# Reordering the start of a two-layer graph attention kernel: weight copies, bias sums and row terms

## The chip, the cores and the metric

The kernel runs on one core of a Trainium2 chip. A core has five engines with instruction streams of their own: TensorE (PE in the profile, its weight loads PEld), VectorE (DVE), ScalarE (ACT), GpSimd (POOL) and SyncE (SP), which here only issues transfers. The metric is device time in microseconds, the median of the runs. An engine runs its instructions in the order in which the built program holds them; that order is made by a scheduler from the order of the source, the tiles' dependencies and the number of buffers, so moving a line in the source can move others too.

## The reference, cut to what matters

Two layers over N = 4096 nodes of width 512. Layer 0 is attention within graphs of 128 nodes, with the dense matrix `adj` added to the scores. Layer 1 is graph attention with 8 heads over the nonzero entries of `adj`.

```python
h = jnp.maximum(_layernorm(x), 0.0)
query = h @ Wq.T + bq;  key = h @ Wk.T + bk;  value = h @ Wv.T + bv
a = jnp.where(mask, query @ key.T * scale, 0.0)
scores = (a + adj + adj) * jnp.where(mask, 1.0, -1000000.0)
x = x + (softmax(scores) * mask) @ value
h = jnp.maximum(_layernorm(x), 0.0)
mx = jnp.einsum('nf,hfd->hnd', h, W)          # layer 1: logits s_i + t_j,
# ... softmax over adj > 0, weighted sum of mx, added to x
```

The kernel folds query and key: `query @ key.T` equals `h M h.T` plus a term for each row and one for each column, with M = Wq.T Wk and with the sums `u` (of Wq and bk), `c` (of Wk and bq) and `z` (of bq and bk). Only M, c, u and z are used afterwards.

## The kernel before

The parts that the change and the prediction touch, with cuts marked. First the folding of the weights:

```python
def fold(sb, tmp, work, ps_t, ps_p):
    wkT_sb = load_weight(tmp, wkT, "wkT_sb", KC, tag="lo")     # four pieces each
    wqT_sb = load_weight(tmp, wqT, "wqT_sb", KC, tag="lo")
    for n, wT in enumerate((wkT_sb, wqT_sb)):
        w = tmp.tile([P, KC, D], F32, name=f"w{n}", tag="lo")
        for k in range(KC):
            pt = ps_t.tile([P, KC, P], F32, name="pt")          # 3 buffers
            for m in range(KC):
                nc.tensor.transpose(pt[:, m, :], wT[:, k, ts(m, P)], ident)   # L174
            dst = w[:, :, ts(k, P)]
            if k % 2: nc.vector.tensor_copy(dst, pt)            # L177
            else:     nc.scalar.copy(dst, pt)                   # L179
    # ...
    for m in range(KC):                                         # M, L190 and L193
        pp = ps_p.tile([P, D], F32, name="pp")                  # 4 buffers
        for k in range(KC):
            nc.tensor.matmul(pp, wq[:, k, ts(m, P)], wk[:, k, :], ...)
        nc.scalar.mul(m_sb[:, m, :], pp, SCALE)
    for n, b in enumerate((bk_sb, bq_sb)):                      # bias rows, L198 and L203
        # pp[:, ts(k, P)] = b[:, k] spread over all partitions, by four products
        row = work.tile([P, D], F32, name=f"b_row{n}", tag="hn")
        nc.scalar.copy(row, pp)
    for dst, wT, row in ((u_col, wqT_sb, rows[0]), (c_sb, wkT_sb, rows[1])):
        for k in range(KC):                                     # bias sums, L208
            nc.vector.scalar_tensor_tensor(wb, wT[:, k, :], SCALE, row, ..., accum_out=dst[:, k:k+1])
    # zp; then u_col spread to u_sb (L218, L222), zp to z_sb (L224, L225)
```

Then the attention loop. It works on groups of two 128-row tiles; `adj` comes in 64 tiles of 128 x 2048 through seven buffers, and each is read by VectorE (a byte mask, L136, stored for layer 1) and by ScalarE (an exponential with a sum, `junk`, L441):

```python
def normed(g):                                  # x -> hT, and the row terms r
    for t in range(G):
        hn = sb.tile([P, D], F32, name="hn")    # 2 buffers; b_row uses the same ones
        norm(xg[g][:, t, :], hn)                # L114, L116, L118, L120, L121
        relu_T(ps_t, hn, hT[:, :, ts(t, P)])    # 4 transposes L127, ScalarE L128
        hu = sb.tile([P, D], BF16, name="hu", bufs=1)
        nc.vector.scalar_tensor_tensor(hu, hn, 0.0, u_sb, ALU.max, ALU.mult,
                                       accum_out=r[:, t : t + 1])      # L394
    nc.gpsimd.tensor_scalar(r, r, z_sb, None, ALU.add)
# before the loop: load_pair(0), wv, bv, adj 0 to 3, load_pair(1), adj 4 to 6;
# normed(0), values(hT, t) L418, read (L136, L441) of group 0, queries(hT) L406, normed(1)
for g in range(NG):
    load_pair(g + 2)                            # x, 3 buffers
    s = scores(g, hT, gT, r, *look)             # L464, exp of s on ScalarE L471
    ngT = queries(nhT)                          # L406
    sT = turned(s)                              # L483, copy to sT on ScalarE L485
    for t in range(G):
        look_on(t)                              # adj of group g + 1
        attend(sT, vs[t], g, t)                 # L491, x1 stored
        nvs.append(values(nhT, t))              # L418
    nhT, nr = normed(g + 2)
# (the last group differs: it prepares layer 1's first rows instead)
```

A stage that prepares layer 1's rows (`project1`, L244) follows, and then 32 aggregations (L284), which take most of the time.

Of the kernel before, what the change touches and what calls it, by code (L numbers as in the profile page):

```python
# [9 lines left out]
F32 = mybir.dt.float32  # L10
# [10 lines left out]
P = 128  # L21
N = 4096
D = 512
NT = N // P
KC = D // P
# [16 lines left out]
SCALE = float(D) ** -0.5  # L42
# [9 lines left out]
def kernel(  # L52
# [22 lines left out]
    nc = tc.nc  # L75
# [11 lines left out]
    ident = const.tile([P, P], F32, name="ident")  # L87
    make_identity(nc, ident)
    one = const.tile([P, 1], F32, name="one")
# [3 lines left out]
    bq_sb = const.tile([P, KC], F32, name="bq_sb")  # L93
    nc.scalar.dma_start(bq_sb, bq)
    bk_sb = const.tile([P, KC], F32, name="bk_sb")
# [15 lines left out]
    def norm(src, hn):  # L111

        stats = small.tile([P, 6], F32, name="stats")
        nc.vector.bn_stats(stats, src)  # L114
        mv = small.tile([P, 2], F32, name="mv")
        nc.vector.bn_aggr(mv, stats)  # L116
        ve = small.tile([P, 1], F32, name="ve")
        nc.gpsimd.tensor_scalar(ve, mv[:, 1:2], EPS, None, ALU.add)  # L118
        rstd = small.tile([P, 1], F32, name="rstd")
        nc.gpsimd.tensor_tensor(rstd, ve, neghalf, ALU.pow)  # L120
        nc.vector.tensor_scalar(hn, src, mv[:, 0:1], rstd, ALU.subtract, ALU.mult)  # L121

    def relu_T(ps_pool, hn, dst):

        pt = ps_pool.tile([P, KC, P], F32, name="pt")
        for k in range(KC):
            nc.tensor.transpose(pt[:, k, :], hn[:, ts(k, P)], ident)  # L127
        nc.scalar.activation(dst, pt, AF.Relu)  # L128
# [11 lines left out]
    def load_weight(pool, src, name, pieces=1, **kw):  # L140
        t = pool.tile([P, KC, D], F32, name=name, **kw)
        n = KC // pieces
        for k in range(0, KC, n):
            nc.sync.dma_start(
                t[:, k : k + n], src[k * P : (k + n) * P].rearrange("(k p) m -> p k m", p=P)
            )
        return t
# [15 lines left out]
    def fold(sb, tmp, work, ps_t, ps_p):  # L163


        wkT_sb = load_weight(tmp, wkT, "wkT_sb", KC, tag="lo")
        wqT_sb = load_weight(tmp, wqT, "wqT_sb", KC, tag="lo")
        nat = []
        for n, wT in enumerate((wkT_sb, wqT_sb)):
            w = tmp.tile([P, KC, D], F32, name=f"w{n}", tag="lo")  # L170
            for k in range(KC):
                pt = ps_t.tile([P, KC, P], F32, name="pt")
                for m in range(KC):
                    nc.tensor.transpose(pt[:, m, :], wT[:, k, ts(m, P)], ident)  # L174
                dst = w[:, :, ts(k, P)]
                if k % 2:
                    nc.vector.tensor_copy(dst, pt)  # L177
                else:
                    nc.scalar.copy(dst, pt)  # L179
            nat.append(w)  # L180
        wk, wq = nat
        m_sb = sb.tile([P, KC, D], F32, name="m_sb")
        c_sb = sb.tile([P, KC], F32, name="c_sb")
        u_col = sb.tile([P, KC], F32, name="u_col")
        u_sb = sb.tile([P, D], F32, name="u_sb")
        z_sb = sb.tile([P, 1], F32, name="z_sb")
        for m in range(KC):
            pp = ps_p.tile([P, D], F32, name="pp")
            for k in range(KC):
                nc.tensor.matmul(  # L190
                    pp, wq[:, k, ts(m, P)], wk[:, k, :], start=(k == 0), stop=(k == KC - 1)
                )
            nc.scalar.mul(m_sb[:, m, :], pp, SCALE)  # L193
        rows = []
        for n, b in enumerate((bk_sb, bq_sb)):
            pp = ps_p.tile([P, D], F32, name="pp")
            for k in range(KC):
                nc.tensor.matmul(  # L198
                    pp[:, ts(k, P)], b[:, k : k + 1].to_broadcast([P, P]), ident,
                    start=True, stop=True,  # L200
                )
            row = work.tile([P, D], F32, name=f"b_row{n}", tag="hn")
            nc.scalar.copy(row, pp)  # L203
            rows.append(row)
        for dst, wT, row in ((u_col, wqT_sb, rows[0]), (c_sb, wkT_sb, rows[1])):
            for k in range(KC):
                wb = work.tile([P, D], BF16, name="wb", tag="hu", bufs=1)
                nc.vector.scalar_tensor_tensor(  # L208
                    wb, wT[:, k, :], SCALE, row, ALU.mult, ALU.mult, accum_out=dst[:, k : k + 1]
                )  # L210
        zk = sb.tile([P, KC], F32, name="zk")
        zp = sb.tile([P, 1], F32, name="zp")
        nc.vector.scalar_tensor_tensor(
            zk, bq_sb, SCALE, bk_sb, ALU.mult, ALU.mult, accum_out=zp
        )
        pp = ps_p.tile([P, D], F32, name="pp")
        for k in range(KC):
            nc.tensor.matmul(  # L218
                pp[:, ts(k, P)], u_col[:, k : k + 1].to_broadcast([P, P]), ident,
                start=True, stop=True,  # L220
            )
        nc.scalar.copy(u_sb, pp)  # L222
        pp = ps_p.tile([P, D], F32, name="pp")
        nc.tensor.matmul(pp[:, :1], zp.to_broadcast([P, P]), one, start=True, stop=True)  # L224
        nc.scalar.copy(z_sb, pp[:, :1])  # L225
        return m_sb, c_sb, u_sb, z_sb

    def split(e, dst):
# [5 lines left out]
    def load_row(pool, i):  # L234
        row = pool.tile([P, D], F32, name="row1")
        nc.sync.dma_start(row, x1_d[ds(i, 1)].rearrange("o p d -> (o p) d"))
        return row
# [104 lines left out]
    with ExitStack() as straight:  # L342
# [4 lines left out]
        with ExitStack() as prep:  # L347
            ps_t = prep.enter_context(tc.tile_pool(name="ps_t0", bufs=3, space=PSUM))
            ps_p = prep.enter_context(tc.tile_pool(name="ps_p0", bufs=4, space=PSUM))
# [28 lines left out]
            with (  # L378
# [5 lines left out]
                def normed(g):  # L384


                    hT = sb.tile([P, KC, G * P], F32, name="hT")
                    r = sb.tile([P, G], F32, name="r", bufs=3)
                    for t in range(G):
                        hn = sb.tile([P, D], F32, name="hn")  # L390
                        norm(xg[g][:, t, :], hn)
                        relu_T(ps_t, hn, hT[:, :, ts(t, P)])
                        hu = sb.tile([P, D], BF16, name="hu", bufs=1)
                        nc.vector.scalar_tensor_tensor(  # L394
                            hu, hn, 0.0, u_sb, ALU.max, ALU.mult, accum_out=r[:, t : t + 1]
                        )
                    nc.gpsimd.tensor_scalar(r, r, z_sb, None, ALU.add)
                    return hT, r
# [105 lines left out]
                NG = NT // G  # L504
                xg, aa = {}, {}
                m_sb, c_sb, u_sb, z_sb = fold(wp, lo, sb, ps_t, ps_p)
                load_pair(0)
                wv = load_weight(wp, wvT, "wv")
# [4 lines left out]
                for k in range(4, AB):  # L513
                    aa[k] = load_adj(ap, k)
                hT, r = normed(0)
                vs = [values(hT, t) for t in range(G)]
                look = seen()
                for t in range(G):
                    look[2].append(read(t, look[0][:, t, :], look[1][t]))
                gT = queries(hT)  # L520
                nhT, nr = normed(1)
                ahead = []
                for g in range(NG):
# [34 lines left out]
                    if g + 2 < NG:  # L558
                        nhT, nr = normed(g + 2)
# [5 lines left out]
            n = len(ahead)  # L565
# [22 lines left out]
        for i in range(NT):  # L588
            row = sb3.tile([P, D], F32, name="row3", bufs=1)
# [29 lines left out]
    with tc.tile_pool(name="ps_ok", bufs=1, space=PSUM) as ps:  # L619
        all_held = small.tile([P, 1], F32, name="all_held")  # L620
        nc.vector.tensor_reduce(all_held, held, AX.X, ALU.min)
        pt = ps.tile([P, P], F32, name="pt_ok")
# [7 lines left out]
    with tc.If(bad > 0):  # L630
# [5 lines left out]
        with (  # L636
# [27 lines left out]
            wq = load_weight(wp, wqT, "wq")  # L664
            wk = load_weight(wp, wkT, "wk")
            wv = load_weight(wp, wvT, "wv")
            with tc.For_i(0, NT, 1) as i:
                row = sb.tile([P, D], F32, name="row")
# [4 lines left out]
                for dst_d, w, b in ((qT_d, wq, bq_sb), (kT_d, wk, bk_sb)):  # L673
                    dst = sb.tile([P, KC, P], F32, name="qk")
                    for m in range(KC):
                        pp = ps_p.tile([P, D], F32, name="pp")
                        for k in range(KC):
                            nc.tensor.matmul(
                                pp[:, :P], w[:, k, ts(m, P)], hT[:, k, :],
                                start=(k == 0), stop=(k == KC - 1),  # L680
# [8 lines left out]
                pp = ps_p.tile([P, D], F32, name="pp")  # L689
# [8 lines left out]
        with (  # L698
# [10 lines left out]
            with tc.For_i(0, NT, 1) as i:  # L709
# [8 lines left out]
                for c in range(N // CW):  # L718
# [12 lines left out]
                    f = sb.tile([P, CW], F32, name="f")  # L731
# [9 lines left out]
                for c in range(N // CW):  # L741
                    v = sb.tile([P, CW // P, D], F32, name="v1")
                    nc.sync.dma_start(v, v_d[:, ts(c, CW // P), :])
                    pt = ps_t.tile([P, KC, P], F32, name="pt")
# [9 lines left out]
                row = sb.tile([P, D], F32, name="row")  # L754
# [7 lines left out]
        with (  # L762
# [13 lines left out]
            with tc.tile_pool(name="ps_m3", bufs=2, space=PSUM) as ps_m:  # L776
                with tc.tile_pool(name="sb3e", bufs=2) as sb, tc.For_i(0, NT, 1) as i:
                    hT = sb.tile([P, KC, P], F32, name="hT1")
                    row = load_row(sb, i)
# [13 lines left out]
                for k in range(KC):  # L793
                    nc.tensor.matmul(
                        pm, hs[:, k : k + 1].to_broadcast([P, P]), w1x[:, k, :D],
                        start=(k == 0), stop=(k == KC - 1),
# [7 lines left out]
            pt = ps_t.tile([P, KC, P], F32, name="pt")  # L804
# [6 lines left out]
                start=True, stop=True,  # L811
# [11 lines left out]
            with tc.For_i(0, n_levels, 1):  # L823
                with (
# [5 lines left out]
                    row = load_row(sb, i)  # L830
# [11 lines left out]
                with (  # L842
# [15 lines left out]
                    row = done[:, ds(i, 1), :].rearrange("p o h -> p (o h)")  # L858
# [48 lines left out]
```

## Time and profile before

| | |
|---|---|
| median of 3 runs | 983.33 us (982.24 to 983.56) |
| span of the profiled run | 981.0 us |
| aggregation, L284 | 489.0 us of TensorE |
| value product, L418 | 116.8 us of TensorE |
| queries, L406 | 113.2 us of TensorE |
| layer 1's projection, L244 | 119.5 us of TensorE |
| transfers | 148.28 MB in all, mean 151 GB/s |

Times in the profile are microseconds from the start of the span. A busy share says how much an engine works, the chain of work says what the end waited for; the timeline shows single instructions, with the idle time before each and what ended it. A float32 product of 128x512 shows as two records. The granted clock is that of TensorE, 1.00 at full speed.

### The profile page before, as it was taken

What the parts mean: (1) busy time and instruction counts of PE and PEld (TensorE: products, weight loads), DVE (VectorE), ACT (ScalarE), POOL (GpSimd) and SP (SyncE); (2) the same over time, 40 slices, a digit from 0 to 9 for tenths busy, and PEclk for the clock granted to TensorE, in tenths of its full rate; (3) what the DMA queues carried; (4) which work ended last, traced back from release to release, by engine and by line L of the source; (5) the groups of instructions that cost most, each with busy time, mean ns of one, the idle gap of its engine ahead of it and who ended that gap; (6) DMA issues with size and microseconds to landing.
All of it is one profiled execution on the core that took longest, in us unless ns stands there. A gap on an engine that the chain in (4) does not pass through costs nothing.

```text
span 981.0 us, 13168 instructions
## 1 busy us (share of the span) xinstructions
PE 947.1 (97%) x5051; PEld 820.8 (84%) x5051; DVE 461.6 (47%) x982; ACT 261.6 (27%) x501; POOL 180.3 (18%) x344
## 2 busy tenths in 40 slices
PE   6899999999999998999999999999999999999995
PEld 4477666766776676888899999999999999999995
DVE  3756866776675287655232423324233242342421
ACT  3676666676671222333100000000000000000000
POOL 1111211221121055555201101011010110101100
PEclk9899999999999998999999999999999999999998
DMA  9949898998992142222013133131221312312111
GB/s 347 419 181 370 352 370 333 377 367 346 368 371 77 59 129 80 65 65 70 6 43 87 50 81 83 47 86 50 80 85 45 86 51 80 86 44 86 50 38 36
DMA packets 58043, 148.28 MB, mean 151 GB/s; under 512 B 6387, under 2 KB 23027, under 8 KB 49779
## 3 DMA queue, kind: packets, MB, share of 16 engines
q1 hardware_dynamic: 48178, 130.31, 38.2%
q10 hardware_dynamic: 9792, 17.05, 4.6%
q8 instruction: 41, 0.67, 0.3%
q14 instruction: 32, 0.25, 0.1%
HBM read 113.77 MB, written 33.55 MB: 150 GB/s over the span
## 4 chain that ended last, share of the span: by engine, by line
PE 86%; DMA 4%; DVE 4%; ACT 3%; POOL 1%; issue 1%; SPq 0%; ACTq 0%; DVEq 0%
PE pg L284 50%; PE pp L418 10%; PE pp L244 9%; PE pp L406 8%; PE pp L491 3%; DMA a<-adj 3%; PE pss L464 2%; PE pt L127 2%; PE pp L190 2%; ACT junk L441 1%; DMA xg<-x 1%; ACT gT L410 1%; POOL part L232 1%; DVE row L121 1%; POOL rstd L120 0%
## 5 line engine op out<-in xcount | busy, mean ns | idle before, releaser
L284 PE MATMUL pg<-part,at 128*128 128x348 f32 x3072 | 489.0, 321 | 1.2 <-DVE e L253 1.2
L284 PEld LDWEIGHTS pg<-part,at 128*128 128x128 f32 x3072 | 488.7, 188 | 1.6 <-issue 1.6
L278 DVE CAST at<-at 128x4096 fp32r<-128x4096 fp8e4 x32 | 73.6, 2301 | 311.6 <-PE pg L284 311.6
L291 ACT COPY tot<-pg 128x522 f32<-128x522 f32 x32 | 19.1, 598 | 469.9 <-PE pg L284 469.9
L441 ACT ACTIVATE junk<-a 128x2048 bf16<-128x2048 f32 (+15 forms) x92 | 124.6, 1355 | 37.4 <-DMA a<-adj 19.4
L244 PE MATMUL pp<-w1x,hT 128*128 128x256 f32 (+1 forms) x512 | 119.5, 387 | 0.0
L418 PE MATMUL pp<-wv,hT 128*128 128x512 f32 x256 | 116.8, 599 | 1.0 <-ACT hT L128 1.0
L406 PE MATMUL pp<-hT,m_sb 128*128 128x256 f32 x512 | 113.2, 379 | 0.0
L244 PEld LDWEIGHTS pp<-w1x,hT 128*128 128x128 f32 x512 | 96.5, 193 | 14.3 <-issue 0.5
L406 PEld LDWEIGHTS pp<-hT,m_sb 128*128 128x128 f32 x512 | 96.1, 190 | 12.9 <-issue 0.5
L418 PEld LDWEIGHTS pp<-wv,hT 128*128 128x128 f32 x256 | 49.1, 193 | 62.0 <-issue 60.4
L136 DVE TENSOR_SCALAR a<-a 128x512 fp8e4<-128x512 f32 x256 | 94.6, 453 | 7.3 <-DMA a<-adj 4.7
L593 POOL COPY den_all<-tot 128x1 f32<-128x1 f32 x31 | 5.8, 186 | 368.2 <-DVE tot L292 368.2
L128 ACT ACTIVATE hT<-pt 128x512 f32<-128x512 f32 x64 | 37.7, 599 | 82.3 <-PE pt L127 82.3
L602 POOL TENSOR_TENSOR tot<-tot,row 128x512 f32<-128x512 f32 x31 | 40.0, 1289 | 62.0 <-DVE tot L297 62.0
L118 POOL TENSOR_SCALAR ve<-mv 128x1 f32<-128x1 f32 x64 | 16.2, 255 | 178.6 <-DVE mv L116 164.8
L232 POOL TENSOR_TENSOR part<-e,part 128x522 fp32r<-128x522 f32 x32 | 42.0, 1312 | 31.4 <-ACT part L231 27.8
L422 DVE TENSOR_TENSOR v<-pp,bv_sb 128x512 f32<-128x512 f32 x32 | 22.1, 691 | 42.3 <-PE pp L418 42.3
L271 DVE STREAM_TRANSPOSE at<-mw 128x1024 f32<-128x1024 f32 x32 | 39.6, 1238 | 0.0
L253 DVE TENSOR_TENSOR e<-pp,e 128x256 f32<-128x256 f32 x64 | 26.7, 418 | 25.3 <-ACT e L372 22.8
L410 ACT ACTIVATE gT<-pp,c_sb 128x256 f32<-128x256 f32 x64 | 29.9, 469 | 31.5 <-PE pp L406 31.4
L120 POOL TENSOR_TENSOR rstd<-ve,neghalf 128x1 f32<-128x1 f32 x64 | 36.8, 578 | 4.6
(94 smaller groups left out, 594.7 us busy)
## 6 DMA issues: line engine op xcount, KB each, us to landing
a<-adj SPq DMA_DIRECT2D x64, 1024.0 KB, 11.9
a_d<-a SPq DMA_DIRECT2D x32, 512.0 KB, 10.2
row<-x_d SPq DMA_DIRECT2D x64, 256.0 KB, 3.4
mw<-a_d SPq DMA_DIRECT2D x128, 128.0 KB, 4.0
xg<-x SPq DMA_DIRECT2D x16, 512.0 KB, 4.6
x_d<-x ACTq DMA_DIRECT2D x32, 256.0 KB, 4.3
out<-tot ACTq DMA_DIRECT2D x31, 256.0 KB, 3.8
wkT_sb<-wkT SPq DMA_DIRECT2D x4, 256.0 KB, 4.6
```

What stands on the lines that cost most here:

```text
L128: nc.scalar.activation(dst, pt, AF.Relu)
L136: nc.vector.tensor_scalar(a8v[:, u], av[:, u], 0.0, None, ALU.is_gt, saturate=False)
L232: nc.gpsimd.tensor_sub(dst[:, :, 1, :], e3, dst[:, :, 0, :].bitcast(F32))
L244: nc.tensor.matmul(pm[g][:, :n], hT[:, k, :], w1x[:, k, g * HW : g * HW + n], start=(k == 0), stop=(k == KC - 1),)
L271: nc.vector.transpose(at8.rearrange("p c n b -> p (c n b)").bitcast(F32).rearrange("p (c u n) -> p c u n", c=NW, n=B), mw.rearrange("p u ( ...
L278: nc.vector.tensor_copy(at.rearrange("p (c b) q -> p c b q", b=BY), at8.rearrange("p c q b -> p c b q"))
L284: nc.tensor.matmul(pg[:, c, : 2 * CW1], at[:, j, :], part(j)[:, c].rearrange("p s w -> p (s w)"), start=(j == 0), stop=(j == NT - 1),)
L406: nc.tensor.matmul(pp[:, : G * P], m_sb[:, k, ts(m, P)], hT[:, k, :], start=(k == 0), stop=(k == KC - 1),)
L410: nc.scalar.activation(gT[:, m, :], pp[:, : G * P], AF.Identity, bias=c_sb[:, m : m + 1])
L418: nc.tensor.matmul(pp, hT[:, k, ts(t, P)], wv[:, k, :], start=(k == 0), stop=(k == KC - 1))
L441: nc.scalar.activation(junk[:, c0:c1], a[:, c0:c1], AF.Exp, scale=2.0 * NEG, accum_out=sums[:, n : n + 1],)
L602: nc.gpsimd.tensor_add(num, num, row)
```

## The change

ScalarE makes all copies of transposed weights, so that VectorE, which must also norm x, holds none of them. The bias rows are spread right after the first four transposes, and the bias sums stand in the source before the weights' product, so that VectorE can make them while TensorE multiplies. u and z are spread inside the product, after two of its four parts. In the loop the row terms `hu` come after the norms of both tiles, so that both norms reach TensorE sooner.

```diff
+        def spread_bias(b):
+            pp = ps_p.tile([P, D], F32, name="pp")
+            for k in range(KC):
+                nc.tensor.matmul(pp[:, ts(k, P)], b[:, k : k + 1].to_broadcast([P, P]), ident, ...)
+            row = work.tile([P, D], F32, name="b_row", tag="hn")
+            nc.scalar.copy(row, pp)
+            return row
...
-                dst = w[:, :, ts(k, P)]
-                if k % 2:
-                    nc.vector.tensor_copy(dst, pt)
-                else:
-                    nc.scalar.copy(dst, pt)
+                nc.scalar.copy(w[:, :, ts(k, P)], pt)
+                if n == 0 and k == 0:
+                    rows = [spread_bias(b) for b in (bk_sb, bq_sb)]
...
-        (the weights' product stood here, before the bias rows; the bias rows after it)
         for dst, wT, row in ((u_col, wqT_sb, rows[0]), (c_sb, wkT_sb, rows[1])):
             ... (bias sums, unchanged; then zp)
-        (u_sb and z_sb were spread here)
+        for m in range(KC):
+            if m == 2:
+                ... (u_sb and z_sb are spread here, with the same instructions)
+            pp = ps_p.tile([P, D], F32, name="pp")
+            for k in range(KC):
+                nc.tensor.matmul(pp, wq[:, k, ts(m, P)], wk[:, k, :], ...)
+            nc.scalar.mul(m_sb[:, m, :], pp, SCALE)
...
+                    hns = []
                     for t in range(G):
                         hn = sb.tile([P, D], F32, name="hn")
                         norm(xg[g][:, t, :], hn)
                         relu_T(ps_t, hn, hT[:, :, ts(t, P)])
+                        hns.append(hn)
+                    for t, hn in enumerate(hns):
                         hu = sb.tile([P, D], BF16, name="hu", bufs=1)
                         nc.vector.scalar_tensor_tensor(hu, hn, 0.0, u_sb, ..., accum_out=r[:, t : t + 1])
```

The two hunks in brackets are told in words; their instructions are those shown under the kernel before.

## Prediction

> **What bounds the kernel now.** I read four views: the page's busy times and its chain of work, a table of stages by windows, the waits of TensorE, and the timeline of the first 60 us.
>
> ```profile
> PE 947.1 (97%) x5051; PEld 820.8 (84%) x5051; DVE 461.6 (47%) x982; ACT 261.6 (27%) x501; POOL 180.3 (18%) x344
> ...
> PE 86%; DMA 4%; DVE 4%; ACT 3%; POOL 1%; issue 1%; SPq 0%; ACTq 0%; DVEq 0%
> ```
>
> The first line is busy time, share of the span and instruction count of each engine, the second the share of each in the chain that ended last. TensorE is the bound for the whole kernel, so a change pays only where TensorE is idle or slow. The stages (busy time of PE, PEld, DVE, ACT and POOL, then granted clock, DMA share, GB/s) show where that is:
>
> ```profile
> 0.00:15.00 15.00, 7.15 (x33) 6.20 (x34) 3.42 (x9) 3.63 (x5) 0.88 (x11) 1.00 0.89 302
> 15.00:31.00 16.00, 16.00 (x40) 7.22 (x39) 8.23 (x23) 10.06 (x14) 4.37 (x11) 0.89 1.02 419
> 31.00:42.00 11.00, 7.58 (x33) 4.96 (x32) 9.92 (x30) 8.81 (x17) 0.63 (x2) 0.73 1.01 420
> 42.00:65.00 23.00, 23.00 (x105) 17.65 (x104) 15.43 (x45) 15.13 (x29) 4.90 (x11) 0.98 0.74 304
> 65.00:345.00 280.00, 275.21 (x1151) 186.78 (x1150) 185.21 (x500) 163.70 (x313) 49.30 (x97) 1.00 0.78 300
> 345.00:395.00 50.00, 44.77 (x203) 36.36 (x202) 38.55 (x79) 13.52 (x30) 26.03 (x48) 0.93 0.35 97
> 395.00:981.00 586.00, 573.40 (x3497) 561.60 (x3495) 200.86 (x302) 46.77 (x96) 94.25 (x166) 0.99 0.22 63
> ```
>
> TensorE idles 7.85 us of the first 15, then 3.42 of the 11 after 31, while it multiplies at 0.73 of its clock; in the 280 us of the attention loop it idles only 4.8. From 42 on there is little to win. The order of the start is in the timeline (start, length, engine, line, operation; in brackets the idle time before it and what ended it):
>
> ```profile
> 12.44 1.29 DVE L114 BATCH_NORM_STATS2 stats<-xg 128x6 f32<-128x512 f32 x2 [6.02 <-DMA xg<-x]
> 13.64 1.27 DVE L177 COPY w<-pt 128x512 f32<-128x512 f32 x2
> 14.37 0.66 PE L174 MATMUL pt<-ident,wqT_sb 128*128 128x128 f32 x4 [2.04 <-DVE w L177]
> 14.87 15.60 PE L190 MATMUL pp<-w,w 128*128 128x512 f32 x32
> 31.39 0.59 ACT L203 COPY b_row<-pp 128x512 f32<-128x512 f32 x1 [0.29 <-PE pp L198]
> 32.01 0.69 DVE L208 SCALAR_TENSOR_TENSOR wb<-wqT_sb,b_row 128x512 bf16<-128x512 f32 x1 [4.06 <-ACT b_row L203]
> 35.79 0.59 ACT L222 COPY u_sb<-pp 128x512 f32<-128x512 f32 x1
> 38.82 2.07 PE L418 MATMUL pp<-wv,hT 128*128 128x512 f32 x2 [0.97 <-ACT hT L128]
> 41.54 6.84 PE L418 MATMUL pp<-wv,hT 128*128 128x512 f32 x14
> ```
>
> Two things are to be seen. VectorE's copies of transposed weights stand behind a bn_stats that waits until 12.44 for x, so TensorE waits 2.04 us for them (VectorE itself had nothing else to do). And after the weights' product (L190, to 30.3) comes a serial tail, bias rows (L198), their sums on VectorE (L208), u (L218), norm, transpose, before the value product (L418) starts at 38.82 and runs steadily only from 41.54.
>
> **What the Trainium skill says.** "TensorE: Matmul & The Clock Gate", section "Part 1: The HAM clock gate", gives half clock as the default, lifted after a busy window of about 3.4 us and imposed again after an idle one. The trace agrees: slices of 1 us show 0.50 at 16 to 19 us, right after the 2.04 us pause, and 0.50 from 37 to 42, in the tail; one record of a 128x512 product takes 0.43 us at full clock (3.43 us for 8 in the loop) and 0.855 at half. "Advanced Engine Details and Errata", section "Sequencer and Instruction Queues", has an engine's instruction wait in its queue for its semaphores; here the VectorE copy that waits behind the bn_stats is the case. Copy length does not decide: a 128x512 copy out of PSUM is 0.59 us on ScalarE and 0.69 on VectorE.
>
> **The change part by part**, with the order in which the built program holds its instructions.
>
> Copies: four go from VectorE to ScalarE. ScalarE then has eight weight copies and two bias rows, at about 0.55 us from start to start where two follow each other (two hT copies take 1.09). The last piece of wq is the limit: its issue at 4.65 plus 6.4 (the longest landing of the four) is 11.1. So the transposes end near 11.7, and the product can start at 11.8 rather than 14.87. The bias rows (16 records, 2.1 us at full clock, about 3.4 at half) fit in the gap before 7.75 when TensorE waits for wk, and nearly cost nothing. With no 2 us pause the product may also escape the half clock of 16 to 19: 32 x 0.43 = 13.8 us instead of 15.4, plus 1.3 us for u and z in its middle. It would end near 27.2 (its third part waits for a buffer freed by ScalarE's first m_sb copy, which stands behind the exponential of adj tile 0, which lands at 17.6, so about 20.2).
>
> That is not what decides. In the new order TensorE does nine hn transposes before the first value product, eight of group 0 and the first of group 1. The ninth needs VectorE, whose order from 12.44 on is: bn_stats pair 1.3, aggregation 0.25; eight sums wb at 0.74, where followed by other work 0.61 (5.5); two hn at 0.46 (0.9); sixteen mask operations at 0.36 (5.8); two row terms hu at about 0.65 (1.3); bn_stats and first aggregation of group 1 (1.4). This is 12.44 + 16.4 = 28.9, and adj tiles (17.6, 20.1, 22.6, 25.1) and u_sb (about 23.9) come in time. From aggregation to hn through GpSimd takes 1.2 us, hn 0.55, the transpose 0.25: the value product starts at about 31.0, 7.8 us before 38.82. TensorE has then idled from 28.3 to 31.0, so the half clock returns for 3.4 to 6.8 us and costs 1.7 to 3.4. The 16 records end at 31.0 + 6.9 + 2.5 = 40.4 against 48.38 before: 8.0 us earlier. Everything behind is TensorE's own work.
>
> Row terms behind both norms, and the loop: the count of operations is unchanged. The order changes. One wait of 1.28 us for hn falls (it belongs to group 2, where VectorE prepares w1x). In return groups 0 and 3 hold no transposes between the turning of s and the value's use, so TensorE sees the whole copy of sT (0.36 us with its handover, 0.6): 2 x 0.6 = 1.2 lost. The waits of 1.32 and 1.19 us for sT stood where ScalarE has an adj tile that is only the second to land after the group's new loads just before sT: groups 7, 9 and 11. In the new order this is so in groups 6, 8, 10 and 12. I put it as 0.6 us lost.
>
> ```profile
> PE pp L491 <- ACT sT L485: 2.8, 3, 1.3
> PE pt L127 <- DVE hn L121: 1.3, 1, 1.3
> ```
>
> (TensorE's waits in the loop: who waits for whom, total, times, longest.) Sum: -8.0 - 1.3 + 1.2 + 0.6 = -7.5. From the end of the loop on the order of every engine is the same, so the 586 us of aggregation stay. 983.3 - 7.5 = 975.8 us; I choose 975.5, since the half clock at 371 to 377 (after a 3.3 us pause in the prepare stage) may fall at a kinder place in its window.
>
> **The rivals.** First: the start is bound by the transfers and nothing is gained. For it: DMA is at 1.02 of its time until 42 us. Against it: VectorE waits only 0.9 to 1.0 us before each of tiles 1 to 3, the queries need no adj tile, and after 58 us the DMA stands still for about 13 us until group 0 frees x's buffer; that slack takes up an 8 us shift. If it held: 983. Second: the loop becomes bound by the adj loads, because it starts 8 us earlier and the slack is gone; the DMA moves 300 GB/s there on average against 420 at the start, and its share is about 0.9 in the busy 200 us. Each new sT wait costs up to 1.3 us; four to six more make 980. Third: the start gains more than I count, because TensorE keeps its full clock through the 2.7 us pause or VectorE reaches the group 1 norm sooner; then 971 to 973.
>
> **Range and chances.** The start gives 6 to 10 us, the loop -2 to +4, the clock's window another 2 either way. A range of 970.5 to 980.5 should hold it 8 times in 10. Over 2% faster means below 963.7, more than all the idle time of the start that can be reached: 0.03. Over 2% slower needs a loop bound by loads throughout: 0.01. Within 2%: 0.96.
>
> **What would show it.** The weights' product starts near 12 and ends near 27; the wait for VectorE's w is gone; the first value product starts at 31, after a pause of 2 to 3 us that is ended by VectorE's hn, and its last record ends near 40; the queries' shift stays about 8 us at 60 and at 345. Sum of sT waits in the loop 2 to 5 us, hn waits none. If the shift shrinks along the loop with sT waits ended by adj, the second rival is right; if the value product starts after 36, my order of VectorE is wrong. A shift at 345 different from that at 981 would mean that the prepare stage or its clock changed, which I don't expect beyond 2 us.

## The result and the profile after

The changed kernel takes 977.25 us (median of 4 runs, 976.57 to 977.26) against 983.44 us (median of 4 runs, 982.24 to 985.37): a ratio of 0.9934, 95% interval 0.9916 to 0.9951, so about 6.2 us or 0.6% faster. The profiled span falls from 981.0 to 975.4 us. In the changed kernel the line numbers are other ones: the weights' transposes are L185, their product is L221, the copy of M out of it L224, the exponential of `adj` L443, the value product L420, the queries L408, the turning of s L485, the copy to sT L487 and the product with sT L493.

Busy times and chain of work, from the page of the changed kernel:

```profile
PE 940.4 (96%) x5051; PEld 816.5 (84%) x5051; DVE 457.6 (47%) x978; ACT 261.5 (27%) x505; POOL 186.6 (19%) x344
...
PE 81%; DMA 8%; DVE 4%; ACT 3%; POOL 1%; issue 1%; SPq 0%; ACTq 0%; DVEq 0%
```

TensorE's busy time fell by 6.7 us with the same 5051 instructions: mostly time that it no longer spent at half clock (17.1 us of the span before, 3.4 now). But in the chain its share went down (86 to 81%) and that of transfers up (4 to 8%): a first sign that somewhere the end now waits for loads. The table of stages, same columns and windows as before:

```profile
0.00:15.00 15.00, 11.09 (x57) 8.21 (x58) 2.85 (x9) 6.83 (x11) 2.05 (x13) 1.00 0.87 304
15.00:31.00 16.00, 13.67 (x46) 7.02 (x45) 14.87 (x44) 13.30 (x21) 7.92 (x11) 0.99 1.02 419
31.00:42.00 11.00, 11.00 (x31) 6.20 (x30) 7.31 (x21) 5.84 (x10) 2.40 (x3) 0.86 1.01 417
...
65.00:345.00 280.00, 271.18 (x1151) 186.65 (x1150) 183.63 (x500) 161.12 (x312) 53.42 (x102) 1.00 0.78 300
345.00:395.00 50.00, 43.58 (x214) 35.90 (x213) 40.38 (x82) 13.81 (x31) 27.78 (x52) 1.00 0.33 94
```

In the first 42 us TensorE idles 6.2 us instead of 11.3, and from 31 to 42 its clock is 0.86 instead of 0.73. In the 280 us from 65 on it idles 8.8 us instead of 4.8: the loop gave some of the gain back. The start in the timeline of the changed kernel:

```profile
11.52 7.03 PE L221 MATMUL pp<-w,w 128*128 128x512 f32 x16
...
19.90 7.13 PE L221 MATMUL pp<-w,w 128*128 128x512 f32 x16 [0.34 <-ACT m_sb L224]
...
29.90 0.33 PE L127 MATMUL pt<-ident,hn 128*128 128x128 f32 x1 [1.99 <-DVE hn L121]
30.07 8.74 PE L420 MATMUL pp<-wv,hT 128*128 128x512 f32 x16
```

The serial tail is gone: the product starts at 11.52 (was 14.87), runs at full clock (16 records in 7.03 us), u is spread in its middle, and the value product follows at 30.07 (was 38.82). The one long pause left, once the first weights have landed, is that of 1.99 us before the ninth transpose. And TensorE's waits in the loop (41 to 345 us), all that the view lists:

```profile
PE pp L493 <- ACT sT L487: 9.0, 8, 2.7
```

Before it was 2.8 us in 3 waits for sT, and 1.3 us in one wait for hn. Milestones of TensorE add it up. The last value record of the start ends at 38.8 instead of 48.4; the first turning of s is at 55.0 instead of 64.7 (9.7 earlier); the first layer 1 projection, at the loop's end, at 337.1 instead of 342.1 (5.0 earlier); the first aggregation at 473.8 instead of 480.3 (6.5 earlier); the last aggregation ends at 963.4 instead of 969.3 (5.9 earlier). So the start gained 9.7, the loop gave back 4.6, the prepare stage added 1.5, and the rest lost 1.0 with the span's tail.

### The profile page after: what moved, and what is told of

Same layout as the page of the kernel before. It is cut to its first block, busy times and chain, and to the rows that moved or that the text cites. A ratio compares the mean times of both kernels' runs of the same rounds, so it can differ in the third digit from the quotient of the medians.

```text
span 975.4 us, 13181 instructions
## 1 busy us (share of the span) xinstructions
PE 940.4 (96%) x5051; PEld 816.5 (84%) x5051; DVE 457.6 (47%) x978; ACT 261.5 (27%) x505; POOL 186.6 (19%) x344
## 2 busy tenths in 40 slices
DMA packets 58042, 148.28 MB, mean 152 GB/s; under 512 B 6386, under 2 KB 23026, under 8 KB 49778
## 4 chain that ended last, share of the span: by engine, by line
PE 81%; DMA 8%; DVE 4%; ACT 3%; POOL 1%; issue 1%; SPq 0%; ACTq 0%; DVEq 0%
PE pg L283 50%; PE pp L420 9%; PE pp L243 8%; PE pp L408 7%; DMA a<-adj 7%; PE pp L493 3%; PE pss L466 2%; PE pt L127 1%; ACT junk L443 1%; ACT gT L412 1%; DMA bv_sb<-bv 1%; DVE row L121 1%; POOL part L231 1%; DVE a L136 1%; POOL rstd L120 1%
## 5 line engine op out<-in xcount | busy, mean ns | idle before, releaser
L443 ACT ACTIVATE junk<-a 128x2048 bf16<-128x2048 f32 (+15 forms) x92 | 124.4, 1353 | 48.9 <-DVE x L495 22.5
L243 PE MATMUL pp<-w1x,hT 128*128 128x256 f32 (+1 forms) x512 | 117.3, 383 | 0.0
L420 PE MATMUL pp<-wv,hT 128*128 128x512 f32 x256 | 116.6, 599 | 0.0
L408 PE MATMUL pp<-hT,m_sb 128*128 128x256 f32 x512 | 113.2, 379 | 0.0
L408 PEld LDWEIGHTS pp<-hT,m_sb 128*128 128x128 f32 x512 | 96.1, 190 | 12.9 <-issue 0.5
L420 PEld LDWEIGHTS pp<-wv,hT 128*128 128x128 f32 x256 | 49.1, 192 | 61.9 <-issue 61.9
L118 POOL TENSOR_SCALAR ve<-mv 128x1 f32<-128x1 f32 x64 | 17.1, 268 | 173.5 <-DVE mv L116 172.0
L493 PE MATMUL pp<-v,sT 128*128 128x512 f32 x64 | 34.4, 618 | 9.4 <-ACT sT L487 9.0
```

What stands on the lines that cost most here:

```text
L243: nc.tensor.matmul(pm[g][:, :n], hT[:, k, :], w1x[:, k, g * HW : g * HW + n], start=(k == 0), stop=(k == KC - 1),)
L408: nc.tensor.matmul(pp[:, : G * P], m_sb[:, k, ts(m, P)], hT[:, k, :], start=(k == 0), stop=(k == KC - 1),)
L420: nc.tensor.matmul(pp, hT[:, k, ts(t, P)], wv[:, k, :], start=(k == 0), stop=(k == KC - 1))
L443: nc.scalar.activation(junk[:, c0:c1], a[:, c0:c1], AF.Exp, scale=2.0 * NEG, accum_out=sums[:, n : n + 1],)
L493: nc.tensor.matmul(po, sT[:, t, :], v, start=True, stop=True)
```

## The experiments

The letters in the expectations: A is the theory that the gain is the start's order and that the loop gives part of it back because ScalarE, in the new order, has an exponential of an `adj` tile, still on its way, in front of the copy to sT; B, that the loop is bound by the loads of `adj` themselves; C, that the row terms' move makes the loop's new waits; D, that x tiles loaded earlier make the `adj` tiles late, which then hold ScalarE or VectorE. Ratios are to the kernel before. Times are medians of all runs; milestones and waits are those of one profiled execution. The first four runs each hold a part of the change.

**Copies alone** (kernel before, the weight copies all on ScalarE):

```diff
-                if k % 2:
-                    nc.vector.tensor_copy(dst, pt)
-                else:
-                    nc.scalar.copy(dst, pt)
+                nc.scalar.copy(w[:, :, ts(k, P)], pt)
```

> The kernel before, with all copies of transposed weights on ScalarE and nothing else of the change. Theory A (the start is a chain on TensorE, and the loop's new waits come with the order that the bias part brings): TensorE's 2.04 us wait for VectorE's copy goes, the product starts near 11.8 and keeps its clock, and 2 to 4 us are saved (979.5 to 981.5); the loop's sT waits stay at 2.8 us in 3. Rival B (the loop is bound by the adj loads, so any earlier start is paid back in it): the start gains the same, but the sT waits grow by as much and the time stays at 983.

979.93 us, ratio 0.9972 (0.9963 to 0.998). The wait for VectorE's w is gone, the weights' product runs from 12.15 at full clock, and the first turning of s is at 60.8, 3.9 us earlier than before. The serial tail stays, and the loop's waits too: 3.0 us for sT and 1.5 for hn. So the copies give about 3 us, and they do not disturb the loop.

**Bias sums first, alone** (kernel before, bias rows and sums, in the source, ahead of the weights' product, u and z after it):

```diff
-        for m in range(KC):      # the weights' product, ahead of the bias rows
-            ...
         rows = []                # bias rows, bias sums, zp
         ...
+        for m in range(KC):      # the weights' product
+            ...
         # u and z spread, as before
```

> The kernel before, with the bias rows and sums placed ahead of the weights' product, u and z behind it, copies and row terms as before. The built order of the loop is that of the changed kernel. Theory A: the product still starts at 14.9 and runs slow to 19, but the value product follows it at about 31.5 instead of 38.8 with no long pause, so 8 us are gained in the start, and about 5 us are lost in the loop (sT waits of about 9 us in groups 6, 8, 10 and 12 and about 0.6 each in 0 and 3): 979 to 981. Rival C (the loop's waits come from the row terms moved behind both norms): the sT waits stay near 3 us, and the time is 974 to 976.

981.02 us, ratio 0.9991 (0.9977 to 1.0005): no gain that stands clear of the noise. In part that was a miss of mine: I had the product start near 14.9, but TensorE's order puts both bias rows and the still present wait for VectorE's w ahead of it. In the timeline it starts at 17.66, behind a bias row that takes 1.92 us at half clock instead of 1.05. Still the first turning of s is at 58.0, 6.7 us earlier than before, because the tail behind the product is gone. Then the loop eats more than half of it, and ends at 339.1, 3.0 us earlier than before; its waits:

```profile
PE pp L491 <- ACT sT L485: 8.0, 8, 2.6
```

Eight waits of 8.0 us, as in the changed kernel, with the row terms in their old place. So it is the move of the bias sums that changes the order of the loop, though not one of its lines is in the loop. The order shows in ScalarE's timeline. In this kernel, as in the changed one, an exponential of an `adj` tile stands in front of the copy to sT, with only one gT between them, in groups 4, 6, 8, 10 and 12; in the kernel before, with the copies alone and with the row terms alone it is groups 2, 5, 7, 9 and 11. How the move reaches the loop (the hn and hu buffers, which the bias part shares with it, are a guess) was not tried and stays open.

**The start without the row terms** (the changed kernel, row terms back in each tile's turn):

```diff
-                    hns = []
-                        hns.append(hn)
-                    for t, hn in enumerate(hns):
```

> The changed kernel, with the row terms put back directly behind each norm. Theory A: the built order of TensorE is the same, so the time is that of the changed kernel within 1 us (976 to 978.5), with sT waits of 8 to 10 us. Rival C: sT waits fall to about 3 us, and the time to 972 or 973.

978.68 us, ratio 0.9956 (0.994 to 0.9972), and a profiled span of 975.4, the changed kernel's. Waits for sT: 8.3 us in 8. The median lies just above the expected 976 to 978.5.

**The row terms alone** (kernel before with those three lines added):

> The kernel before, with only the row terms moved behind both norms. Theory A: the start and the loop keep their order on TensorE; the 1.28 us wait for hn in group 2 may go, nothing else: 981.5 to 983.5. Rival C: the sT waits grow from 2.8 to about 9 us, and the time to about 988.

981.88 us, ratio 0.9989 (0.9978 to 1.0). The wait for hn is gone, as it was meant; sT waits are 4.0 us in 6, so 1.2 us more than before. The two runs agree: the row terms are worth 0 to 2 us (1.2 and 1.4 by the medians), and most of the loop's new waits come without them. C falls.

**The copy to sT on VectorE** (changed kernel):

```diff
-                    nc.scalar.copy(sT, ps)
+                    nc.vector.tensor_copy(sT, ps)
```

> The changed kernel, with the copy of the turned scores (sT) on VectorE instead of ScalarE. Theory A (sT waits only because ScalarE, in order, has an adj tile that hasn't landed in front of it): the waits of TensorE for sT fall from 9.0 us to 3 or less, and the time to about 971 (970 to 973). Rival B (the loop is bound by the adj loads themselves): as many waits appear elsewhere in the loop, and the time stays within 1.5 us of 977.

975.39 us, ratio 0.9926 (0.991 to 0.9943). The waits hardly fell, they changed their owner (two more of 1.0 us together are left out):

```profile
PE pp L493 <- DVE sT L487: 7.2, 8, 2.2
```

I had expected at most 3 us. VectorE runs in order, too, and other work of its own stands in front of the copy. Two places from its timeline, in the groups that TensorE had turned at 185.14 and 300.92:

```profile
184.75 2.82 DVE L136 TENSOR_SCALAR a<-a 128x512 fp8e4<-128x512 f32 x8 [0.71 <-DMA a_d<-a]
187.46 0.42 DVE L487 COPY sT<-pss 128x256 f32<-128x256 f32 x1
...
303.00 0.55 DVE L121 TENSOR_SCALAR row<-row,mv,rstd 128x512 f32<-128x512 f32 x1 [0.98 <-POOL rstd L120]
303.46 0.42 DVE L487 COPY sT<-pss 128x256 f32<-128x256 f32 x1
```

At the first place eight byte masks run one behind the other, held up by the store of an earlier mask and not by a load. The second, with the longest wait of 2.2 us, is behind the norms of layer 1's rows. So this run doesn't tell A from B: it only put other work in front of the copy. The loop became 2.0 us shorter.

**No exponentials of `adj`** (changed kernel; it leaves out ScalarE's reads of all row tiles but the first four, so the softmax sums of the others are incomplete; loads, masks and stores all stay):

```diff
-                            if c0 < c1:
+                            if c0 < c1 and i < 2 * G:
```

> The changed kernel, which leaves out ScalarE's exponentials of adj for all row tiles but the first four, so the softmax sums lack the other graphs' part. All loads, masks and stores stay. Theory A: only the 0.6 us gaps of the groups without transposes between the turning and the use remain, sT waits are 1 to 2 us, and the time is about 970 (968 to 971). Rival B: the masks on VectorE still need every tile, so buffers and loads set the same pace, and the time stays above 975.

969.24 us, ratio 0.9867 (0.9846 to 0.9887). The loop ends at 328.7 instead of 337.1, and of its waits two are left:

```profile
PE pp L493 <- ACT sT L487: 1.2, 2, 0.6
```

They are those of groups 0 and 3, where nothing stands between the turning and the use. The first turning of s is 1.0 us earlier here, so the loop itself is 7.4 us shorter. All transfers are still there (148.26 MB instead of 148.28), so it isn't the loads alone that bound it: B falls as a bound. But the run also takes about 100 us of work from ScalarE (in the loop it is busy for 59.7 us instead of 162.9) and one of the readers from each buffer, so it doesn't yet tell a late tile from a ScalarE that is merely full. The value products below do, with ScalarE's work unchanged.

**The second x pair first** (changed kernel, `load_pair(1)` right behind `load_pair(0)`, against the pause of 1.99 us):

> The changed kernel, with the second pair of x tiles loaded right behind the first, ahead of all adj tiles. Theory A for the start (the value product's start is held by the ninth transpose, which waits on VectorE for the norm of group 1): VectorE makes that norm earlier, TensorE's pause of 1.99 us shrinks to below 1, the half clock behind it goes, and 2 to 4 us are saved (973.5 to 975.5). Rival D (adj tiles land 1.3 us later, and ScalarE or VectorE are held by them): 976.5 to 978.

976.79 us, ratio 0.9938 (0.9918 to 0.9957), the same as the changed kernel. The timeline of this kernel shows why:

```profile
21.87 7.13 PE L221 MATMUL pp<-w,w 128*128 128x512 f32 x16 [1.66 <-ACT m_sb L224]
...
30.15 0.33 PE L127 MATMUL pt<-ident,hn 128*128 128x128 f32 x1 [0.28 <-DVE hn L121]
```

The pause before the ninth transpose shrank from 1.99 to 0.28 us, but tile 0 of `adj` lands later: ScalarE's exponential of it starts at 19.44 instead of 17.47 and holds up the first copy of M, and the product's second half waits 1.66 instead of 0.34. So D is right for the start. The value product starts at 30.54, later than the 30.07 of the changed kernel; it ran at full clock here (7.13 us), so the first turning is still 1.1 us earlier (53.88), but 3.4 us at half clock came in the loop instead, behind a wait of 2.69 us for sT.

**Both** (copy to sT on VectorE and second x pair first):

> The changed kernel with sT copied by VectorE and the second pair of x tiles loaded first. If both reasons hold and don't meet, the gains add: 967 to 970. If the earlier start meets the loads (rival B), no faster than the better of the two alone.

975.65 us, ratio 0.9923 (0.9906 to 0.9939): the two do not add, it is the time of the first of them alone. That is the number given for rival B, but it doesn't speak for the loads: the second x pair had gained nothing that could be added.

**Value products first** (changed kernel; in the loop each tile's value product, which needs no sT, stands ahead of the product with sT):

```diff
                         look_on(t)
-                        attend(sT, vs[t], g, t)
-                        prepare_on()
                         if not last:
                             nvs.append(values(nhT, t))
+                        attend(sT, vs[t], g, t)
+                        prepare_on()
```

> The changed kernel, and in the loop each tile's value product stands in the source ahead of the product that uses sT, so that TensorE has 3.4 us of work between the turning of s and its use in every group. Theory A (the loop gave back about 4.6 us because ScalarE holds an adj tile in front of the sT copy, and TensorE has nothing to do in the meantime): the eight sT waits of 9.0 us, the longest 2.7, are all shorter than 3.4 us and vanish; the loop's first layer 1 projection comes about 8 to 9 us earlier than 337.1, and the time is 967 to 970. Rival B (the loop is bound by the adj loads, and a wait that is covered comes back elsewhere in the loop): the waits move to other operands, hn or hT or adj's successors, the loop ends at 334 or later and the time is 974 to 977.

967.05 us (964.51 to 970.71), ratio 0.9846 (0.9823 to 0.987): the best of all, 10.2 us below the changed kernel. The loop ends at 324.4 instead of 337.1 (12.7 us earlier, where 8 to 9 were expected), and of the eight waits for sT none is left; a new one stands in the last group, which has no value product:

```profile
PE pp L408 <- ACT hT L128: 0.9, 2, 0.5
PE pp L493 <- ACT sT L487: 0.5, 1, 0.5
```

The late copies of the changed kernel and the reason for them are shown by ScalarE's timeline of the changed kernel in group 10, where TensorE had turned s at 246.84:

```profile
248.11 1.91 ACT L443 ACTIVATE junk<-a 128x2048 bf16<-128x2048 f32 x1 [2.32 <-DMA a<-adj]
...
250.37 0.36 ACT L487 COPY sT<-pss 128x256 f32<-128x256 f32 x1
```

ScalarE idles 2.32 us for a tile of `adj`, though s is turned and its copy would take 0.36 us; the copy comes at 250.37, and TensorE, whose eight transposes of hn are done by 248.1, stands still:

```profile
247.06 1.04 PE L127 MATMUL pt<-ident,hn 128*128 128x128 f32 x8
250.79 1.13 PE L493 MATMUL pp<-v,sT 128*128 128x512 f32 x2 [2.69 <-ACT sT L487]
```

The Trainium skill ("Advanced Engine Details and Errata", section "Sequencer and Instruction Queues") has an instruction pushed into its engine's queue, where it waits for its semaphores. The trace agrees: what stood behind the waiting one did not start, at a price of 2.7 us here. With the value products first, TensorE has a product of 3.4 us between turning and use. In the new kernel the group turned at 182.52 has a late tile in front of the copy in the same way:

```profile
182.73 3.60 PE L420 MATMUL pp<-wv,hT 128*128 128x512 f32 x8
183.73 1.91 ACT L443 ACTIVATE junk<-a 128x2048 bf16<-128x2048 f32 x1 [2.27 <-DMA a<-adj]
186.00 0.36 ACT L487 COPY sT<-pss 128x256 f32<-128x256 f32 x1
186.41 1.12 PE L493 MATMUL pp<-v,sT 128*128 128x512 f32 x2
```

ScalarE idles 2.27 us for the tile and copies 3.5 us after the turning, as in group 10 above, but TensorE works until 186.33 and the product with sT follows 0.08 us later. The exchange also changed ScalarE's order in part: in groups 6, 8 and 10 the exponentials that had held up the copy now stand behind it. So the gain is that of both, and the lines above show the covering by itself.

From the first turning to the loop's end it takes 271.2 us instead of 282.1. That is 10.8 us, more than the 9.0 of listed waits, because groups without a listed wait also got shorter: 18.38 us (127.39 to 145.77) instead of 18.70 (92.95 to 111.65). Most of these 0.32 us are waits for sT, too, which the view doesn't list. In the changed kernel such a group has only five transposes to cover the copy:

```profile
93.17 0.71 PE L127 MATMUL pt<-ident,hn 128*128 128x128 f32 x5
93.94 1.13 PE L493 MATMUL pp<-v,sT 128*128 128x512 f32 x2
```

The transposes start 0.11 us apart, so the product could have started at 93.72; ScalarE's copy (93.53, 0.36 us long) ends at 93.89, and the product starts at 93.94. The modelled end of the last transpose, 93.88, hides these 0.2 us. The remaining 0.1 is between the product's two records, for a reason that I did not find. Another 1.8 us came in the start, where the value product ran at full clock this time.

**Value products first in the kernel before** (the same exchange and nothing else):

> The kernel before with the same exchange alone, the start and the row terms as before. Theory A: only its 4.06 us of sT waits can go, so the loop ends at 337 to 338.5 instead of 342.1 and the time is 978 to 980; the distance to the changed kernel with the exchange is then the whole gain of the start, 9 to 11 us in place of 6.2. Rival B: the start's gain is partly lost in the loop whatever the order, the distance between the two stays near 6, and this kernel is at 973 to 976 or at 983.

975.43 us (973.5 to 977.76), ratio 0.9921 (0.9898 to 0.9944); the loop ends at 335.6. I expected 978 to 980, since 4.1 us of listed waits were all there was to win (2.8 for sT and 1.3 for hn; the expectation calls all of it sT); the loop became 7.2 us shorter, again by the groups' 18.38 us. B's figure for this kernel was met, but not its mechanism: the two loops now take nearly the same (270.2 and 271.2 us). Here, too, the late tile is covered: in the group turned at 250.01 ScalarE idles 2.18 us for its tile and copies at 253.41, and no wait of TensorE is marked.

The two kernels lie 8.4 us apart by the medians (975.43 to 967.05), and further apart in their profiled executions: 12.3 at the first turning (65.44 to 53.16), 11.2 at the loop's end, 10.6 in the spans. Part of that is the clock: in this profile of the kernel before, the first six records of the weights' product are 0.85 us apart instead of 0.43. So the loop now gives back 1.0 us of the start's gain, where it gave back 4.6 in the change as made, and more than 6.2 us reach the end. A's 9 to 11 holds for the spans, and is slightly missed by the medians.

## Why the prediction was right, step by step

- **The start's order: right.** Product from 11.5 (said 11.8) to 27.0 (said 27.2), no wait for VectorE's w, no half clock at 16 to 19. The m_sb wait was short, 0.34. The value product at 30.07 (said 31.0) after a pause of 1.99 us (said 2 to 3) ended by VectorE's hn. That order of VectorE was the limit is confirmed by the second x pair: with its data there earlier, the pause goes.
- **The half clock after the pause: right here, and chance.** The value product took 8.74 us, 1.7 more than the 7.04 that it takes at full clock in other runs; I had put 1.7 to 3.4, and reckoned with 6.9 + 2.5 = 9.4. These 0.7 us and the start of the product 0.9 earlier make the start's term 9.6 us instead of 8.0.
- **hn waits in the loop: right.** None is left; the row terms alone remove it as well.
- **Groups 0 and 3: right.** Two waits of 0.61 us, 1.2 in all, as said.
- **The sT waits of the other groups: the term that was mis-sized.** I said "I put it as 0.6 us lost", and a sum of 2 to 5 us. It is 9.0 us; without groups 0 and 3 it is 7.8, where before had 2.8: 5.0 lost instead of 0.6. The places were right: groups 6, 8, 10 and 12 wait, with 1.48, 1.44, 2.69 and 1.07 us, and groups 4 and 7 add 0.26 and 0.81, which I had not counted. The mistake was to charge the old price for each place. In group 9 of before the tile in front landed 0.32 us ahead of the turning and the wait was 1.19 us; in group 10 of after it landed 1.19 us behind the turning and the wait was 2.69. A tile further ahead counts as well: in group 12 the exponential in front of the copy starts at 286.62 without idle time, but behind one that had idled 1.53 us for its tile. I had counted places in the order and not looked at the landings, though before showed already that a place has no fixed price: of its groups 7, 9 and 11 the last has no listed wait (its third, of 0.27 us, is in group 5).
- **The prepare stage and the aggregation: within what I allowed.** The stage gave 1.5 us: the half clock did not come this time (below), which is worth at most 3.4, and TensorE's waits for the rows grew from 5.2 to 6.4 us. The aggregations lost 0.6.
- **The sum.** -9.7 for the start, +4.6 for the loop, -1.5 and +1.0 behind it make -5.6 in the span. The prediction had -8.0, +0.5 and nothing: its errors of -1.7 in the start, +4.1 in the loop and -0.5 behind it partly cancel. That the time came out so much better than the loop's term did is luck.
- **The rivals.** The first (nothing gained at the start) is wrong by 9.7 us. The second (loop bound by loads) had the right symptom, more sT waits with `adj` behind them, and the wrong cause: with the loads untouched and only the order changed, the time is 967. The third (start gains more) is partly what happened, and the loop hid it.

## What to carry to other kernels

A gain at the front counts in full only if the next stage's waits do not grow, so look at each wait of that stage in the new order, and at when the data of the instruction in front lands, not at its place alone. When an engine's in-order queue has something that waits for a transfer in front of a short copy that the bounding engine needs, moving the copy to another engine may only change the owner of the wait; giving the bounding engine independent work between producing and using (here 3.4 us of value products) removed it, and was worth more than the whole change. And a reordering in one place can reorder another (moving the bias sums alone took the loop's sT waits from 2.8 to 8.0 us), so compare the built orders everywhere.

## What the runs showed of the hardware that I had not expected

The same pause may or may not bring the half clock. In the prepare stage TensorE waits 3.3 us for VectorE's row in before and in after, and in the window from 345 to 395 us the clock was 0.93 before (the line is in the prediction) and 1.00 after (above). 0.93 over 50 us is about 7 us at half clock; by slices of 1 us it was 6.8. After had none, and the other kernels here 0, 3.4 or 6.8, after pauses of 3.1 to 3.3. Likewise the pause of 1.99 us before the value product was followed by 3.4 us of half clock in the changed kernel (8.74 us) and by none in the one with sT on VectorE (7.04 us). The Trainium skill ("TensorE: Matmul & The Clock Gate", section "Part 1: The HAM clock gate") says that the activity window of about 3.4 us runs freely, and that the moment of warming up therefore depends on where in the window the first product falls. Stretches of 0, 3.4 and 6.8 us agree with that, for the return to half clock as well. It gives an idle window of about 3.4 us as what brings the half clock; here it followed pauses of 1.99 us, and of 2.04 in the kernel before, so a pause need not be that long. The agreement that the prediction saw is with the length of the stretches and not with the length of the pause. At half clock, 3.4 us of work cost 1.7. So each such pause can cost 0 to 3.4 us by chance, as much as most single steps of the change are worth, and executions of one and the same kernel differ by it as well: the mean granted clock of the kernel before is 0.987 to 0.991 in the ten runs beside the copy on VectorE, where one stretch of 3.4 us makes less than 0.002.
